# Sums of k over the tokens: 32x32 block transposes and a matmul of 8 columns in place of a matmul of 256 columns

## The chip, the cores and the metric

The kernel runs on one core of one Trainium2 chip, in float32. The metric is the device time of one execution in microseconds (us). Of the kernel before, four runs gave a median of 1077.0 us. One more execution was profiled, and all readings of the profile below are from that one.

## The reference

One transformer block over x of shape (16, 512, 256): 16 sequences, which the kernel calls batches, of 512 tokens with 256 features. A layer norm feeds a linear attention with 16 heads of 16 features and, beside it, a mixture of experts (a shared SwiGLU network, and two of eight experts for each token).

```python
x = L0_attn_inputs_q
xn = _layernorm(x, axis=-1)
...
q = _feature_map(q)          # elu(x) + 1
k = _feature_map(k)
kv = jnp.einsum('bkhd,bkhm->bhdm', k, v)
out = jnp.einsum('bqhd,bhdm->bqhm', q, kv)
normalizer = jnp.einsum('bqhd,bkhd->bqh', q, k)
normalizer = jnp.maximum(normalizer, EPS)
out = out / normalizer[..., None]
...
x = x + attention(xn) + ffn(xn)
```

The normalizer needs, for each batch, the sum of k over its 512 tokens: 256 numbers. These are the "sums of k" of the title. The same 256 numbers also carry the bias of v into kv.

## The kernel before, in words

Tokens lie on the 128 partitions: a batch is four tiles of 128 tokens by 256 features, so `kk` (the keys after the feature map) is 128x4x256. The loop over the 16 batches is software-pipelined by hand. In the body for batch b the program text has: `front(b+1)` (projections of k and q, feature maps, routing), `summarize(b)` (the products of k and the normalized x), `normalize(b+2)`, `hidden_rows(b)` (first layer of the routed experts, line 424), then `key_sum(b+1)` and `attend(b+1)`, `hidden(b)` (first layer of the shared network, line 443), `mix(b)` and `gather(b)` (lines 482 to 535). Batch 0 has its own `front`, `key_sum` and `attend` ahead of that. After the loop 67 or more tiles of tokens, sorted by their pair of experts, are fetched by indirect DMAs and multiplied with the experts' second layer (line 703).

Each engine executes its own instructions strictly in one order, and that order is fixed when the program is built: a scheduler places instructions by the order of the program text, by what it reckons to be ready, and by free buffers. An instruction whose inputs come late is therefore found behind others that stand after it in the text. Matmul results go to a pool of six PSUM buffers (`ps_mm`); a buffer is free again when VectorE or ScalarE has read it.

The sums of k are made in `key_sum` (lines 453 to 462). GpSimd adds the four token tiles to one of 128x256 (lines 456 and 457, tile `k2`). TensorE multiplies it with a 128x128 matrix of ones (line 459, tile `pks`), which adds over the 128 partitions and leaves the 256 sums on each of the 128 partitions. VectorE copies the result out of PSUM (line 461, tile `ksb`). `ksb` has two readers: `attend` (line 510), which divides q by the normalizer, writes it to memory (line 522) and reads it back in blocks for a transpose (lines 236 and 242), and `mix` (line 489). All the elementwise work of the routing (lines 346 to 414) and the evictions of the hidden layers (lines 432 and 450) are on VectorE too.

A float32 matmul appears in the profile as two TensorE instructions, each with its own load of the 128x128 weights: the 16 matmuls of line 459 are 32 entries.

Of the kernel before, what the change touches and what calls it, by code (L numbers as in the profile page):

```python
# [10 lines left out]
FP = mybir.dt.float32  # L11
AF = mybir.ActivationFunctionType
ALU = mybir.AluOpType
AX = mybir.AxisListType

P = 128
# [5 lines left out]
def block_kernel(  # L22
# [29 lines left out]
    nc = tc.nc  # L52
    B, S, D = x.shape
# [28 lines left out]
    const = ctx.enter_context(tc.tile_pool(name="const", bufs=1))  # L82
# [5 lines left out]
    small = ctx.enter_context(tc.tile_pool(name="small", bufs=2))  # L88
    dram = ctx.enter_context(tc.tile_pool(name="dram", bufs=1, space=bass.MemoryType.DRAM))
    ps_mm = ctx.enter_context(tc.tile_pool(name="ps_mm", bufs=6, space=bass.MemoryType.PSUM))  # L90
# [20 lines left out]
    Q = 32  # L111
    NQ = P // Q
# [7 lines left out]
    ident = const.tile([P, P], FP)  # L120
# [47 lines left out]
    def load_expert(i):  # L168
# [9 lines left out]
    ones = const.tile([P, P], FP)  # L178
# [6 lines left out]
    nc.gpsimd.affine_select(  # L185
        out=headmask, in_=headmask, pattern=[[DH, P // DH], [0, DH]],
        compare_op=ALU.is_ge, fill=0.0, base=DH - 1, channel_multiplier=-1,
    )

    before = const.tile([P, P], FP)  # L190
# [262 lines left out]
    def key_sum(b, kk):  # L453

        k2 = one.tile([P, 2, D], FP, tag="k2", name=f"k2_{b}")
        nc.gpsimd.tensor_tensor(k2, kk[:, 0:2, :], kk[:, 2:4, :], ALU.add)  # L456
        nc.gpsimd.tensor_tensor(k2[:, 0, :], k2[:, 0, :], k2[:, 1, :], ALU.add)
        pks = ps_mm.tile([P, D], FP, tag="mm", name=f"pks_{b}")
        nc.tensor.matmul(pks, lhsT=ones, rhs=k2[:, 0, :], start=True, stop=True)  # L459
        ksb = work.tile([P, D], FP, tag="ksb", name=f"ksb_{b}")  # L460
        nc.vector.tensor_copy(ksb, pks)
        return ksb

    def summarize(b, xn, kk):
# [275 lines left out]
    for b in range(B):  # L740
# [12 lines left out]
        if b == 0:  # L753
            sums = key_sum(0, kk)
            queries[0] = attend(0, qq, sums)
# [7 lines left out]
        if b + 1 < B:  # L763
            sums = key_sum(b + 1, fronts[b + 1][2])
            queries[b + 1] = attend(b + 1, fronts[b + 1][1], sums)
# [17 lines left out]
    n = nc.values_load(  # L783
        filled, min_val=TT, max_val=TILES,
        skip_runtime_bounds_check_because="whole tiles for all tokens, a part of a tile more for a pair",
    )
# [58 lines left out]
```

## Time and profile before

| what | value |
|---|---|
| median of 4 runs (lowest, highest) | 1077.0 us (1074.64, 1081.7) |
| profiled execution, whole | 1078.83 us |
| its span, first to last instruction | 1077.1 us |
| mean granted TensorE clock | 0.997 of full speed |
| PE (matmul) busy | 1053.5 us, 98% of the span |
| PEld (weight load) busy | 625.7 us, 58% |
| DVE (VectorE) busy | 662.1 us, 61%, 1744 instructions |
| ACT (ScalarE) busy | 376.0 us, 35% |
| POOL (GpSimd) busy | 243.9 us, 23% |

PE is the TensorE's matmul row and PEld its weight loads, which run beside the matmuls. Matmuls are pipelined: the duration of one (592 ns with 512 columns, 379 ns with 256) contains a latency that overlaps with the next, so that what one costs is read from the distance to the next one's start or from the chain of waits, not from its duration. "issue" in a list of waits is idle time for which the profile shows no cause.

### The profile page before, as it was taken

How to read it: one execution, taken by the hardware profiler on the slowest of the kernel's cores; microseconds unless marked ns; L12 is line 12 of the kernel's file. 1: busy time of each engine (PE TensorE's matmuls, PEld its weight loads, DVE VectorE, ACT ScalarE, POOL GpSimd, SP SyncE). 2: the span in 40 equal slices, each digit the busy share in tenths (PEclk: the TensorE clock that was granted, in tenths of full speed). 3: DMA queues.
4: the chain of work that ended last, by engine and by line, in shares of the span. 5: the costliest groups of instructions: out<-in, count | busy, mean ns of one | idle time of the engine just before them, and what ended most of it. 6: DMA issues, size and time to landing. Idle time of an engine off the chain costs nothing.

```text
span 1077.1 us, 11307 instructions
## 1 busy us (share of the span) xinstructions
PE 1053.5 (98%) x3404; PEld 625.7 (58%) x3404; DVE 662.1 (61%) x1744; ACT 376.0 (35%) x703; POOL 243.9 (23%) x313
## 2 busy tenths in 40 slices
PE   6999999999999999999999999999999999999996
PEld 5565747475757566665757474757566444444442
DVE  7948475565647474747474655646386576666663
ACT  3412231322232231313131322212112686777771
POOL 6102021010202020201011110102002665555552
PEclk9999999999999999999999999999999999999998
DMA  7343332424334242423232313031212654454440
GB/s 229 99 118 111 85 123 74 137 59 137 96 100 126 81 137 63 142 59 98 68 109 59 117 40 118 31 106 50 73 55 88 206 175 151 152 154 151 148 153 29
DMA packets 129054, 116.02 MB, mean 108 GB/s; under 512 B 72109, under 2 KB 113597, under 8 KB 128736
## 3 DMA queue, kind: packets, MB, share of 16 engines
q1 hardware_dynamic: 119120, 77.16, 23.7%
q0 software_dynamic: 9456, 37.59, 11.1%
q8 instruction: 29, 0.48, 0.2%
q10 hardware_dynamic: 416, 0.52, 0.2%
q14 instruction: 33, 0.27, 0.1%
HBM read 65.36 MB, written 50.27 MB: 107 GB/s over the span
## 4 chain that ended last, share of the span: by engine, by line
PE 94%; DVE 2%; DMA 1%; issue 1%; POOL 0%; ACT 0%; SPq 0%; POOLq 0%; DVEq 0%
PE phr L424 20%; PE phs L443 20%; PE py L703 19%; PE po L534 15%; PE pk L312 6%; PE pxk L469 5%; PE pq L323 5%; PE pm L499 2%; PE pvk L482 1%; PE pks L459 1%; DMA xn_all<-h_d,source 0%; DMA x<-in_x 0%; DMA kk_all<-h_d,source 0%; DMA qq_all<-h_d,source 0%; DVE hT L680 0%
## 5 line engine op out<-in xcount | busy, mean ns | idle before, releaser
L703 PE MATMUL py<-w_sb,hT 128*128 x536 | 230.5, 592 | 2.0 <-DVE hT L686 2.0
L443 PE MATMUL phs<-xnT,win_sb 128*128 128x512 f32 x512 | 223.6, 593 | 0.0
L424 PE MATMUL phr<-w_sb,xnT 128*128 128x512 f32 x512 | 222.8, 592 | 0.0
L703 PEld LDWEIGHTS py<-w_sb,hT 128*128 128x128 f32 x536 | 101.7, 190 | 130.5 <-issue 129.3
L424 PEld LDWEIGHTS phr<-w_sb,xnT 128*128 128x128 f32 x512 | 97.1, 190 | 114.7 <-issue 106.0
L443 PEld LDWEIGHTS phs<-xnT,win_sb 128*128 128x128 f32 x512 | 96.8, 190 | 113.2 <-issue 110.5
L292 POOL TENSOR_TENSOR res<-x,bo_sb 128x1024 f32<-128x1024 f32 x16 | 37.8, 2366 | 433.2 <-DMA h_d<-res 287.7
L534 PE MATMUL po<-wout_sb,hs_all 128*128 128x256 f32 x512 | 123.6, 379 | 0.0
L535 DVE TENSOR_TENSOR res<-po,res 128x256 f32<-128x256 f32 x64 | 27.2, 424 | 131.8 <-PE po L534 131.8
L534 PEld LDWEIGHTS po<-wout_sb,hs_all 128*128 128x128 f32 x512 | 96.1, 190 | 12.4
L450 DVE TENSOR_TENSOR hs_all<-phs,sa_hs 128x512 f32<-128x512 f32 x64 | 43.6, 681 | 91.8 <-PE phs L443 86.5
L449 ACT ACTIVATE sa_hs<-phs 128x512 f32<-128x512 f32 x64 | 38.2, 597 | 159.7 <-PE phs L443 154.4
L717 POOL DMA_INDIRECT out<-y,goal x67 | 67.6, 1009 | 76.3 <-DVE y L714 65.1
L301 ACT ACTIVATE km<-km 128x1024 f32<-128x1024 f32 x16 | 16.9, 1057 | 177.9 <-DVE km L300 177.9
L432 DVE TENSOR_TENSOR hr<-phr,sa_hr 128x512 f32<-128x512 f32 x64 | 43.8, 685 | 55.8 <-PE phr L424 32.8
L430 ACT ACTIVATE sa_hr<-phr 128x512 f32<-128x512 f32 x64 | 38.0, 597 | 99.1 <-PE phr L424 90.3
L534 PE MATMUL po<-kvo,qT 128*128 128x256 f32 x256 | 67.0, 384 | 0.0
L312 PE MATMUL pk<-wkr_sb,xnT 128*128 128x266 f32 x256 | 62.1, 396 | 3.9 <-DVE qq_all L327 2.3
L469 PE MATMUL pxk<-kk_all,xn_all 128*128 128x256 f32 x256 | 57.9, 379 | 0.0
L323 PE MATMUL pq<-wq_sb,xnT 128*128 128x256 f32 x256 | 57.8, 379 | 0.0
L312 PEld LDWEIGHTS pk<-wkr_sb,xnT 128*128 128x128 f32 x256 | 49.7, 195 | 13.6 <-ACT xnT L283 2.4
L456 POOL TENSOR_TENSOR k<-kk_all 128x512 f32<-128x512 f32 x16 | 27.6, 1727 | 130.4 <-DVE sm L358 126.6
(148 smaller groups left out, 1262.9 us busy)
## 6 DMA issues: line engine op xcount, KB each, us to landing
h_d<-hr SPq DMA_DIRECT2D x64, 256.0 KB, 2.5
h_d<-res SPq DMA_DIRECT2D x64, 129.0 KB, 1.8
q_d<-qq_all SPq DMA_DIRECT2D x16, 512.0 KB, 2.8
qb<-q_d SPq DMA_DIRECT2D x64, 128.0 KB, 2.6
w_sb<-in_w SPq DMA_DIRECT2D x64, 128.0 KB, 3.4
x<-in_x SPq DMA_DIRECT2D x15, 512.0 KB, 4.1
xn_d<-xn_all SPq DMA_DIRECT2D x14, 512.0 KB, 3.0
xb<-xn_d SPq DMA_DIRECT2D x56, 128.0 KB, 3.1
```

Source lines behind the costliest of these rows:

```text
L312: nc.tensor.matmul(pk, lhsT=xnT[:, k, ts(t, P)], rhs=wkr_sb[:, k, :], start=(k == 0), stop=(k == KD - 1),)
L323: nc.tensor.matmul(pq[:, t, :], lhsT=xnT[:, k, ts(t2 + t, P)], rhs=wq_sb[:, k, :], start=(k == 0), stop=(k == KD - 1),)
L424: nc.tensor.matmul(ph, lhsT=xnT[:, k, ts(t, P)], rhs=w1_sb[:, k, ts(half, HID)], start=(k == 0), stop=(k == KD - 1),)
L430: nc.scalar.activation(sa, halves[0], AF.Silu)
L432: nc.vector.tensor_tensor(hr, halves[1], sa, ALU.mult)
L443: nc.tensor.matmul(ph, lhsT=win_sb[:, k, ts(half * KH + f, P)], rhs=xnT[:, k, :], start=(k == 0), stop=(k == KD - 1),)
L449: nc.scalar.activation(sa, halves[0], AF.Silu)
L450: nc.vector.tensor_tensor(h[:, f, :], halves[1], sa, ALU.mult)
L469: nc.tensor.matmul(pxk[:, c, :], lhsT=xn[:, t, ts(c, P)], rhs=kk[:, t, :], start=(t == 0), stop=(t == NT - 1),)
L534: nc.tensor.matmul(po, lhsT=a, rhs=w, start=(i == 0), stop=(i == len(parts) - 1))
L703: nc.tensor.matmul(py.rearrange("p j d -> p (j d)"), lhsT=self.hT[:, f, ts(j, P)], rhs=w2_sb[:, f, bass.ds(regs[i % TR], 2 * D)], start=(f ...
L717: stored = nc.gpsimd.indirect_dma_start(out=out_rows, out_offset=bass.IndirectOffsetOnAxis(ap=self.goal[:, i : i + 1], axis=0), in_=y, in_ ...
```

## The change

`key_sum` adds over the partitions in another way. VectorE transposes each 32x32 block of the 128x256 tile (8 blocks in each of 4 groups of 32 partitions, which are called quadrants here): afterwards partition j of a quadrant holds, for each block n, the 32 tokens of that quadrant for feature 32n+j. VectorE adds these 32 and gets 128x8. A matmul with a constant 0/1 matrix `fold` (128x128, one where row and column agree modulo 32) adds the four quadrants and leaves the result in all four: 8 columns in place of 256. VectorE copies these 8 columns out of PSUM and then spreads them with a second block transpose, whose source repeats each column 32 times, to the same 128x256 tile `ksb` as before. `fold` is made once, at the start, by VectorE from the identity matrix.

```diff
+    fold = const.tile([P, P], FP)
+    nc.vector.tensor_reduce(fold[:, 0:Q], ident.rearrange("p (a j) -> p j a", j=Q), AX.X, ALU.add)
+    nc.vector.tensor_copy(
+        fold[:, Q:].rearrange("p (a j) -> p a j", j=Q), fold[:, 0:Q].unsqueeze(1).to_broadcast([P, NQ - 1, Q])
+    )
...
         nc.gpsimd.tensor_tensor(k2[:, 0, :], k2[:, 0, :], k2[:, 1, :], ALU.add)
-        pks = ps_mm.tile([P, D], FP, tag="mm", name=f"pks_{b}")
-        nc.tensor.matmul(pks, lhsT=ones, rhs=k2[:, 0, :], start=True, stop=True)
+        N = D // Q
+        nc.vector.transpose(
+            k2[:, 1, :].rearrange("p (n j) -> p n j", j=Q), k2[:, 0, :].rearrange("p (n j) -> p n j", j=Q)
+        )
+        kq = small.tile([P, 2, N], FP, tag="kq", name=f"kq_{b}")
+        nc.vector.tensor_reduce(
+            kq[:, 0, :], k2[:, 1, :].rearrange("p (n j) -> p n j", j=Q), AX.X, ALU.add
+        )
+        pks = ps_mm.tile([P, N], FP, tag="mm", name=f"pks_{b}")
+        nc.tensor.matmul(pks, lhsT=fold, rhs=kq[:, 0, :], start=True, stop=True)
+        nc.vector.tensor_copy(kq[:, 1, :], pks)
         ksb = work.tile([P, D], FP, tag="ksb", name=f"ksb_{b}")
-        nc.vector.tensor_copy(ksb, pks)
+        nc.vector.transpose(
+            ksb.rearrange("p (n j) -> p n j", j=Q), kq[:, 1, :].unsqueeze(2).to_broadcast([P, N, Q])
+        )
```

Here P is 128, D is 256, Q is 32 and NQ is 4. Nothing else of the kernel is edited.

## The prediction

> **What bounds the kernel now.** I read the page's chain of waits first, then the chain in order of time over one batch, then single instructions around the matmul that is replaced. The page's chain, by engine and by line, and two rows of the 40 slices:
>
> ```profile
> PE   6999999999999999999999999999999999999996
> DVE  7948475565647474747474655646386576666663
> ...
> PE 94%; DVE 2%; DMA 1%; issue 1%; POOL 0%; ACT 0%; SPq 0%; POOLq 0%; DVEq 0%
> PE phr L424 20%; PE phs L443 20%; PE py L703 19%; PE po L534 15%; PE pk L312 6%; PE pxk L469 5%; PE pq L323 5%; PE pm L499 2%; PE pvk L482 1%; PE pks L459 1%; DMA xn_all<-h_d,source 0%; DMA x<-in_x 0%; DMA kk_all<-h_d,source 0%; DMA qq_all<-h_d,source 0%; DVE hT L680 0%
> ```
>
> TensorE sets the end, and between the first slice and the last it has no visible hole: the busy times by stage give 704.00 us of 704.00 from 76 to 780 us. The idle time is at the start (9.6 us of the first 33 and 1.7 us at 73 us) and after 800 us. The replaced matmul, line 459, is a link of the chain. In order of time (start, duration, what):
>
> ```profile
> 136.27 13.73 PE phr L424 x32
> 150.00 0.43 PE pks L459 x2
> 150.43 13.73 PE phs L443 x32
> 164.16 0.89 PE pvk L482 x8
> ```
>
> It takes 0.431 us of TensorE per batch (two entries; 16 entries of 256 columns on line 323 take 3.45 us, 0.2156 each), 16 x 0.431 = 6.9 us in all. That is the most the change could win on TensorE. VectorE is busy 61% and has about 20 us free in each steady batch (31.13 us busy of 50.75 from 125.80 to 176.55).
>
> **What is saved on TensorE.** Eight columns don't cost an eighth of 32: weights are loaded for each entry. The nearest row is the routing's short matmul with 12 columns, once in the kernel, between matmuls of 256 columns:
>
> ```profile
> 785.26 0.41 PEld L545 LDWEIGHTS pc<-total,before 128*128 128x128 f32 x2
> 785.48 0.29 PE L545 MATMUL pc<-total,before 128*128 128x12 f32 x2
> 785.59 0.30 PEld L546 LDWEIGHTS pc<-total,ones 128*128 128x128 f32 x2
> 785.62 0.37 PE L546 MATMUL pc<-total,ones 128*128 128x12 f32 x2
> 785.81 0.52 PEld L469 LDWEIGHTS pxk<-kk_all,xn_all 128*128 128x128 f32 x3
> ```
>
> Weight loads of 0.19 us start at 785.48, 785.59, 785.70 (the second of the two that begin at 785.59) and 785.81: 0.11 us apart, with nothing long enough in between to hide them. The chain gives the four matmuls 0.12 + 0.22 us, and the 16 of line 469 behind them 3.55 us where others take 3.45, so 0.44 us for four, again 0.11 each. Line 482 above agrees: 8 entries of 128 columns in 0.89 us. A pair of 8 columns: 0.22 us. Bounds: 0.11, if one of the two loads is hidden after all, and 0.43, if it is no shorter than now. I take 0.22, by the row that it is nearest to. The saving is 16 x (0.431 - 0.22) = **3.4 us**, with ends of 0 and 5.1.
>
> [...]
>
> **What is added on VectorE**, per batch, with these rows (busy us, mean ns, then idle time before it):
>
> ```profile
> L512 DVE TENSOR_REDUCE rz<-qk 128x64 f32<-128x1024 f32 x16 | 19.4, 1214 | 0.4
> L686 DVE STREAM_TRANSPOSE hT<-hb 128x256 f32<-128x256 f32 x99 | 37.1, 420 | 6.4 <-ACT hb L673 5.3
> L317 DVE TENSOR_TENSOR lg<-pk,bkr_sb 128x10 f32<-128x10 f32 x64 | 10.0, 156 | 0.0
> L461 DVE COPY ksb<-pks 128x256 f32<-128x256 f32 x16 | 6.6, 415 | 6.2 <-PE pks L459 6.2
> L410 DVE TENSOR_REDUCE res<-parts 128x4 f32<-128x48 f32 x32 | 4.9, 195 | 0.0
> ```
>
> Two transposes of 128x256: 0.42 each; the second reads a repeated column, which no row shows, between 0.15 (a short instruction) and 1.24 (line 242, four times the size), taken at 0.42. The reduction of 256 numbers, between line 410 (48 in, 195 ns) and line 512 (1024 in, 1214 ns): 195 + 208 x 1019/976 = 412 ns. The copy of 8 columns from PSUM: 0.16 (10 columns, line 317). Less the old copy, 0.415. Sum 0.42 + 0.41 + 0.16 + 0.42 - 0.415 = **1.00 us per batch, 16 us in all**; VectorE goes from 662 to 678 us. Cost on the path: nothing, because some 20 us per batch are free there; if VectorE set the pace, it would be all 16 us.
>
> [...] One operation becomes four, one a reduction. If VectorE bounded the kernel, the sum would be 16 - 3.4 = 12.5 us slower by it; the chain above, 94% PE and 2% DVE, says that it doesn't.
>
> **The new wait.** The matmul used to need only GpSimd's sum; now it also waits for VectorE's transpose and reduction. Behind it on TensorE stand the 32 entries of line 443, and behind those all the rest, so any lateness goes straight to the end. How much room is there? Around the same link of the chain (start, duration, engine, line; last bracket: idle before it):
>
> ```profile
> 138.85 0.72 POOL L457 TENSOR_TENSOR k<-k 128x256 f32<-128x256 f32 x1
> ...
> 146.67 0.69 DVE L432 TENSOR_TENSOR hr<-phr,sa_hr 128x512 f32<-128x512 f32 x1 [0.20 <-PE phr L424]
> 150.47 0.42 DVE L461 COPY ksb<-pks 128x256 f32<-128x256 f32 x1 [3.10 <-PE pks L459]
> ```
>
> GpSimd's sum is there at 139.6, the matmul starts at 149.84. VectorE is full until 147.36 and then idle for 3.1 us: the two new operations (0.83 us) fit there with 1.6 us to spare. A batch later there is more: sum at 188.61, VectorE idle from 194.69 to 197.44, matmul at 200.60. VectorE's order is not the text's (the statistics of line 263 stand between evictions of line 432 that precede or follow them at will), so I expect such holes to be used. Cost 0, ends 0 and 1.9 us per batch (first rival).
>
> After the matmul the result is about 0.2 us later than before (0.16 + 0.42 against 0.415). Line 510 and the write of q (157.00 in this batch) move by that and by up to 0.8 us of the new operations; behind the write on SP's queue stand the four reads of line 236 (159.78), which land some 2.6 us after the last is issued, by 164.3, and are first used by the transpose of line 242 at 182.97: 18 us of cover. The PSUM buffer of `pks` comes free earlier, after a copy of 0.16 instead of 0.415.
>
> **The start.** `fold` costs a reduction of 128 numbers (0.28 by the same line) and a copy (0.2; at most 0.42) on VectorE, once. VectorE is idle until 2.85 us and again 0.78 and 0.87 us before its next two statistics, each waiting for x; the identity is ready at 2.75. Cost 0, at most 0.5. For batch 0 there is less cover: VectorE has no hole above 0.4 us from 6 to 57 us. There the copy of line 461 starts only at 35.98 though its matmul ran from 32.45 to 32.88. If the matmul kept its place and the two operations stood where the copy stands, TensorE would wait from 32.45 to 36.8, 4.4 us; if it moves behind some matmuls of line 424, nothing. PSUM buffers are another cover: at 46.62 TensorE needs one that line 432 frees at 44.3, so a VectorE that is 1 us later still frees it in time, one 2.3 us later doesn't. I take 0.5, ends 0 and 4.4.
>
> **Sum**: -3.4 + 0.5 = -2.9 us against the profiled span: 1077.1 becomes 1074.2, its execution 1078.83 becomes 1075.9. That execution stands 1.8 us above the median of the four runs; the same difference on the median gives 1077.0 - 2.9 = **1074.1 us**. The four runs spread from 1074.64 to 1081.7, 0.65%, so I count less than 0.5% (5.4 us) as no change.
>
> **Rivals.**
>
> Slower: the two VectorE operations stand behind the last eviction of line 432 while the matmul keeps its place. In the batch with the matmul at 200.60 that eviction ends at 201.55, the two operations at 202.4 and the matmul starts at about 202.5: 1.9 us of idle TensorE, 16 x 1.9 - 3.4 = +27 us, **1104 us**. It decides from 0.55 us per batch on, (5.4 + 3.4)/16. For it: in that batch the copy of line 461 stands just behind that eviction. Against it: the operations' input is there 12 us earlier, and one scheduler places both queues, which would put the matmul behind some of line 443.
>
> No gain: the first batch costs 2 to 4.4 us as worked out above and eats the saving: -3.4 + 3.4 = **1077 us**. For it the solid VectorE row at the start, against it that TensorE had other work to go on with (line 424).
>
> Faster than I say: one load of each pair hides (-5.1), and a shifted order closes the hole of 1.67 us before 74.78, where TensorE waits for a transpose of line 242 that stands behind an eviction of line 535: -6.8, **1070.2 us**. The four short matmuls at 785 us speak against the first half.
>
> The change doesn't do what it says: the short pair takes as long as the long one: **1077 us**. The spacing of 0.11 us speaks against it.
>
> **How the numbers follow.** Forecast 0.57, slower rival 0.14, no gain 0.13, faster rival 0.13, no shorter matmul 0.03. Faster by over 0.5% is the faster rival, 0.13; slower is the slower rival, 0.14; the other three cases, 0.73, are within. The range of 8 in 10 goes from 1070 (the faster rival's time) to 1082 (where the slower rival begins to count) and leaves out that rival and half of the faster one. The likeliest case alone: 1072 to 1076.
>
> **What would show it.** Right: the pair of line 459's successor takes about 0.22 us in the chain, the period from one batch's line 424 to the next's shrinks from 50.76 to about 50.55 us, and DVE busy rises by 16 us with PE as full as before. Wrong: idle time of PE or PEld before `pks` put down to the new reduction; a first matmul of line 424 later than 32.9 us; a pair at 0.43 us; or a batch period that grows.

## The result, and the profile after

| | before | after |
|---|---|---|
| median of the timed runs | 1078.05 us (71 runs) | 1079.78 us (44 runs) |
| lowest to highest | 1074.05 to 1082.69 | 1078.01 to 1082.7 |
| profiled execution, span | 1078.83, 1077.1 us | 1081.27, 1079.5 us |
| granted TensorE clock, profiled | 0.997 | 0.994 |
| DVE busy, instructions | 662.1 us, 1744 | 672.8 us, 1794 |

The ratio is 1.0019, with a 95% interval from 1.001 to 1.0027: slower by 1.1 to 2.9 us, where 2.9 us less were forecast. Less than 0.5%, and on the other side. The medians hide a change of form. Before, 32 of 71 runs lie below 1077; after, none of 44 lies below 1078.0. The slow end has not moved. The short times have gone.

The profile of after, the page's chain of waits by engine:

```profile
PE 92%; DVE 4%; DMA 2%; issue 1%; POOL 1%; SPq 0%; ACT 0%; POOLq 0%; DVEq 0%
```

TensorE still sets the end, but VectorE has gone from 2% to 4% of the chain. The chain of waits in order of time shows where. First one steady batch (start, duration, what):

```profile
141.29 13.73 PE phr L430 x32
155.03 0.12 PE pks L475 x2
155.15 13.84 PE phs L449 x32
168.98 0.89 PE pvk L501 x8
```

The short pair costs 0.12 us, and the 32 matmuls behind it 13.84 instead of 13.73: 0.23 us in all against 0.43 before. The period from one batch to the next goes from 50.76 to 50.55 us (`phr` starts at 242.24, 292.79 and 343.34). This is the forecast saving, and it is there in every steady batch.

The loss is all in the first 80 us. TensorE's timeline there, before and then after (start, duration, engine, line, tiles, shapes, count; last bracket: idle time before it and what ended it):

```profile
21.71 3.83 PE L312 MATMUL pk<-wkr_sb,xnT 128*128 128x266 f32 x16 [2.25 <-DVE qq_all L327]
25.38 3.62 PE L323 MATMUL pq<-wq_sb,xnT 128*128 128x256 f32 x16
28.83 3.62 PE L469 MATMUL pxk<-kk_all,xn_all 128*128 128x256 f32 x16
32.29 0.59 PE L459 MATMUL pks<-k,ones 128*128 128x256 f32 x2
32.72 13.90 PE L424 MATMUL phr<-w_sb,xnT 128*128 128x512 f32 x32
```

```profile
21.81 5.51 PE L318 MATMUL pk<-wkr_sb,xnT 128*128 128x266 f32 x16 [2.76 <-DVE qq_all L333]
27.16 3.62 PE L329 MATMUL pq<-wq_sb,xnT 128*128 128x256 f32 x16
30.61 3.62 PE L488 MATMUL pxk<-kk_all,xn_all 128*128 128x256 f32 x16
36.17 0.36 PE L475 MATMUL pks<-kq,fold 128*128 128x8 f32 x2 [1.94 <-DVE kq L471]
36.38 15.68 PE L430 MATMUL phr<-w_sb,xnT 128*128 128x512 f32 x32
```

Three differences: the 16 matmuls `pk` take 5.51 instead of 3.83 us, there is a wait of 1.94 us in front of `pks` for the new reduction, and the 32 matmuls `phr` take 15.68 instead of 13.90. They add to 0.1 + 1.7 + 1.9 + 1.8 = 5.5, less 0.2 for each of the two short pairs in that stretch. At the first `pk` of batch 2 the kernel is 80.01 - 74.78 = 5.2 us late. At `phr` of batch 14 it is 747.77 - 745.42 = 2.35 late: the 13 pairs in between won back 2.9, 0.22 each. The span ends 2.4 late.

The two longer groups are matmuls at half clock. Two windows of after (stretch, its length, busy time and instructions of PE, PEld, DVE, ACT and POOL, granted clock, DMA share, GB/s):

```profile
22.80:26.20 3.40, 3.40 (x9) 2.64 (x8) 3.40 (x11) 1.06 (x1) 2.54 (x2) 0.50 0.43 149
36.50:40.00 3.50, 3.50 (x6) 1.47 (x6) 3.48 (x11) 0.94 (x1) 2.45 (x2) 0.52 0.00 0
```

Each of the two holes is followed by 3.4 us at a granted clock of 0.50, which costs half of that, 1.7 us. PE is "busy" throughout, so neither its busy time (1053.3 us) nor its 98% shows anything. Before has the clock at 1.00 in both places. Only the second of the two belongs to the change, though: the first hole and a half clock behind it are found below in a kernel with the old matmuls too, so that 1.7 of the 5.2 us are luck of this pair of executions. The mean clock tells the same: 2 x 1.7 / 1079.5 = 0.003, which is 0.997 against 0.994.

Why is the reduction late? The chain of after, in order of time, just before the wait:

```profile
34.26 0.60 DVE qm L306
34.86 0.10 DVE ex L355
34.96 0.08 DVE ex L358
35.04 0.35 DVE k L467
35.39 0.31 DVE st L269
35.70 0.33 DVE kq L471
36.03 0.14 issue
36.17 0.36 PE pks L475 x2
```

GpSimd's sum, the transpose's input, is ready at 26.1 us. The transpose (L467) starts 8.9 us later. It stands on VectorE behind routing of the first batch and evictions and feature maps of the second, and VectorE has only one gap there, of 0.45 us.

### The profile page after: what moved, and what is told of

Same layout as the page of the kernel before. It is cut to its first block, busy times and chain, and to the rows that moved or that the text cites. A ratio compares the mean times of both kernels' runs of the same rounds, so it can differ in the third digit from the quotient of the medians.

```text
span 1079.5 us, 11287 instructions
## 1 busy us (share of the span) xinstructions
PE 1053.3 (98%) x3404; PEld 625.5 (58%) x3404; DVE 672.8 (62%) x1794; ACT 376.2 (35%) x703; POOL 244.9 (23%) x313
## 4 chain that ended last, share of the span: by engine, by line
PE 92%; DVE 4%; DMA 2%; issue 1%; POOL 1%; SPq 0%; ACT 0%; POOLq 0%; DVEq 0%
PE phr L430 20%; PE phs L449 20%; PE py L722 19%; PE po L553 15%; PE pxk L488 5%; PE pk L318 5%; PE pq L329 4%; PE pm L518 1%; PE pvk L501 1%; DMA x<-in_x 1%; DMA xn_all<-h_d,source 0%; DMA kk_all<-h_d,source 0%; DMA qq_all<-h_d,source 0%; DVE hT L699 0%; POOL qq_all L673 0%
```

## The experiments

The theory: all of the loss is in batch 0, where the matmul now waits for a full VectorE queue; the wait itself and the half clock behind it cost more than the 16 short pairs save. Rivals: the loss comes from the later batches (shifted order, more VectorE work), or from `fold` at the start. The first four kernels ran on one chip (before there: median 1083.27 us of 30 runs), the other four on another (before there: 1077.2 us of 35 runs), and each ratio is against before on the same chip.

**Batch 0 in the old form, the rest in the new one.**

```diff
+        if b > 0:
...
+        else:
+            pks = ps_mm.tile([P, D], FP, tag="mm", name=f"pks_{b}")
+            nc.tensor.matmul(pks, lhsT=ones, rhs=k2[:, 0, :], start=True, stop=True)
+            ksb = work.tile([P, D], FP, tag="ksb", name=f"ksb_{b}")
+            nc.vector.tensor_copy(ksb, pks)
```

> Batch 0 adds over the partitions by the matrix of ones as before, batches 1 to 15 in the new way. Theory A (the loss is TensorE's wait for the reduction of batch 0 and the half clock behind it; every later batch gains 0.2 us): no idle time before the first matmul of pks, the first matmul of phr at about 33 us, time 3.0 us below the kernel before (15 x 0.2), ratio about 0.997. Rival B (the 16 us more on VectorE, or the making of fold at the start, cost the time): ratio at or above 1.000, and the lateness is there without the wait.

Measured: 1078.79 us (12 runs), ratio 0.9967, interval 0.9948 to 0.9985. The loss is gone and the saving shows. So the later batches aren't where the time is lost, nor is `fold`, which is still made here. One thing shows up that had been hidden: `pks` of batch 1 waits 0.86 us for its reduction. After has no wait there, with TensorE some 6 us later at that point.

**Only batch 0 in the new form.**

```diff
-        if b > 0:
+        if b == 0:
```

> Only batch 0 adds in the new way, batches 1 to 15 as before. Theory A: the whole loss and almost none of the gain: TensorE idle some 1.9 us before the first pks, a half clock of 3.4 us after it in most runs (1.7 us), so 4 to 5.5 us above the kernel before, ratio 1.004 to 1.005. Rival B: the time of the kernel before or 1 us more.

Measured: 1090.1 us (7 runs), ratio 1.0058, interval 1.0033 to 1.0083, so 3.6 to 9 us for a single matmul. The two ratios multiplied give 0.9967 x 1.0058 = 1.0025, the changed kernel's own (1.0019 and, on the second chip, 1.0024): within their intervals, the two parts make up the whole. TensorE's timeline of this kernel:

```profile
27.07 3.62 PE L494 MATMUL pxk<-kk_all,xn_all 128*128 128x256 f32 x16
35.29 0.57 PE L476 MATMUL pks<-kq,fold 128*128 128x8 f32 x2 [4.61 <-DVE kq L472]
35.71 16.32 PE L430 MATMUL phr<-w_sb,xnT 128*128 128x512 f32 x32
```

TensorE is 3.5 us earlier than in after (`pxk` at 27.07, not 30.61), because the first hole was only 0.53 us in this run. It gains little: the reduction lets `pks` start only 0.9 us earlier, so the wait grows to 4.61 us, and the 32 `phr` behind it, at half clock at first (0.65 granted from 35.7 to 42.5 us, 1.00 from there to 50), take 16.32 instead of 13.90 us. What TensorE gains at the start is lost again at this wait.

**All batches new, the first sum and its matmul moved behind half of `phr`.** `hidden_rows` calls a function between its second and third token tile, which makes the sum and `attend` of batch 0.

```diff
         for t in range(NT):
+            if t == 2:
+                halfway()
...
-        if b == 0:
-            sums = key_sum(0, kk)
-            queries[0] = attend(0, qq, sums)
...
+        def halfway():
+            if b == 0:
+                first.append(key_sum(0, kk))
+                queries[0] = attend(0, qq, first[0])
```

> All batches in the new way, but the sums and the normalizer of batch 0 stand behind the second token tile of its hidden rows in the program text, so that TensorE has four matmul groups of phr to do before it needs the reduction. Theory A: no idle time before the first pks, ratio about 0.997, the same as with batch 0 in the old way. Rival B: no change against the changed kernel, 1.002. A third way, that the later normalizer of batch 0 makes its q late: idle time before the po matmuls of batch 0, ratio above 1.000.

Measured: 1080.68 us (12 runs), ratio 0.9976, interval 0.9956 to 0.9996. With all 16 sums in the new form the kernel is faster than before, by 0.4 to 4.8 us, once TensorE has something to do in place of the wait. TensorE's timeline:

```profile
33.95 7.03 PE L432 MATMUL phr<-w_sb,xnT 128*128 128x512 f32 x16
40.81 0.28 PE L477 MATMUL pks<-kq,fold 128*128 128x8 f32 x2
40.95 7.11 PE L432 MATMUL phr<-w_sb,xnT 128*128 128x512 f32 x16
```

`phr` starts right behind `pxk`, no idle time stands ahead of `pks`, and the 32 `phr` take 14 us, not 15.7. The first hole (2.33 us) and its half clock (`pk` takes 5.52 us) are still there.

**The changed kernel, with the hole in front of `pks` filled.** Four unused matmuls, 8 entries, are added between `pxk` and `pks` in batch 0; their results are read by nobody. `last_pxk`, not shown, holds the last matmul of `pxk`.

```diff
...
+        if b == 0:
+            pw = ps_mm.tile([P, D], FP, tag="mm", name="pw")
+            with tc.issue_after(last_pxk[0].ins):
+                for _ in range(4):
+                    nc.tensor.matmul(pw, lhsT=ident, rhs=xn_all[:, 0, 0, :], start=True, stop=True)
```

> The changed kernel with four extra matmuls of 256 columns (1.7 us, their result is not used) between the last pxk and the first pks of batch 0: TensorE works through the time in which it would be idle. If idle TensorE is followed by a half clock, as the trace of the changed kernel suggests, the clock stays full in the window of 34 to 40 us, the 32 matmuls of phr of batch 0 take 13.7 us instead of 15.5, and the time falls by up to 1.7 us against the changed kernel: ratio to the kernel before 1.000 to 1.001. If the half clock has another cause, it stays at 1.002.

Measured: 1083.84 us (12 runs), ratio 1.0012, interval 0.9988 to 1.0037. The interval holds both the changed kernel's ratio and one below 1, so the time tells nothing. The trace does, first TensorE's timeline and then the window of `phr`:

```profile
34.79 1.89 PE L480 MATMUL pw<-xn_all,ident 128*128 128x256 f32 x8
36.90 0.36 PE L482 MATMUL pks<-kq,fold 128*128 128x8 f32 x2 [0.21 <-DVE kq L473]
37.11 13.98 PE L430 MATMUL phr<-w_sb,xnT 128*128 128x512 f32 x32
```

```profile
37.00:51.00 14.00, 14.00 (x34) 6.09 (x34) 13.99 (x53) 7.08 (x9) 3.80 (x7) 1.00 0.21 77
```

With the hole filled and nothing else changed, the clock stays at 1.00 and `phr` takes 13.98 instead of 15.68 us. So in this execution no half clock followed. Alone that doesn't show the idle time to be the cause, because the last kernel of this section has a hole of 1.90 us and no half clock behind it either; what tells the cases apart is worked out in the next section.

**Before, with `fold` added and nothing else.** Its result is read by nobody.

```diff
+    fold = const.tile([P, P], FP)
+    nc.vector.tensor_reduce(fold[:, 0:Q], ident.rearrange("p (a j) -> p j a", j=Q), AX.X, ALU.add)
+    nc.vector.tensor_copy(
+        fold[:, Q:].rearrange("p (a j) -> p a j", j=Q), fold[:, 0:Q].unsqueeze(1).to_broadcast([P, NQ - 1, Q])
+    )
```

> The kernel before, and beside it the two VectorE operations that make fold (not used for anything). Theory A: they stand between the statistics and the normalization of batch 1, 0.5 us where TensorE is still busy with q of batch 0, and cost nothing: ratio 0.999 to 1.001. Rival B (making fold at the start is what costs): ratio 1.002 or more and a longer idle time of TensorE before the keys of batch 1.

Measured: 1077.78 us (12 runs), ratio 0.9996, interval 0.9976 to 1.0015: no cost that can be measured. The profiled execution, 1082.23 us, has a first hole of 3.95 us, and the `pk` behind it take 6.66 instead of 3.83 us (granted clock 0.50 from 22 to 28 us), though all its matmuls are the old ones. Before has the hole without `fold` (2.25 us), and here VectorE had also waited 1.78 us for the x of batch 1. So the first hole isn't the change's doing.

**Batches 0 and 1 old, 2 to 15 new.**

```diff
+        if b > 1:
...
+        else:
```

The program text also makes `fold` later here, behind `normalize(1)`, and so does that of the next kernel. On VectorE it stands where it stood, between the statistics and the normalization of batch 1 (10.73 us here, 11.39 in after).

> Batches 0 and 1 in the old way, 2 to 15 in the new one. Theory A: also the 0.9 us that TensorE waited for the reduction of batch 1 when only batch 0 was old is gone; 14 x 0.2 = 2.8 us gained, no idle time before any pks, ratio about 0.996 to 0.997. Rival B: not below 1.000.

Measured: 1073.56 us (12 runs, nine of them from 1072.21 to 1074.32), ratio 0.9971, interval 0.9955 to 0.9987. It beats both kernels: 3.6 us less than before and 6.6 us less than the changed kernel on the same chip, from giving up two of 16 savings. In the profiled execution (1072.21 us, span 1070.4) there is no first hole, and `phr` starts at 29.03 us:

```profile
18.09 3.77 PE L313 MATMUL pk<-wkr_sb,xnT 128*128 128x266 f32 x16
...
29.03 13.90 PE L425 MATMUL phr<-w_sb,xnT 128*128 128x512 f32 x32
```

Against before's span that is 32.72 - 29.03 = 3.7 us from the start and 14 x 0.21 = 2.9 from the short pairs: 6.6 of the 6.7 us. The first part comes from this execution having no first hole, which the edit isn't shown to bring about: the medians differ by 3.6 us, not 6.7.

**The same, and GpSimd's residual of batches 0 and 1 issued behind their routing.** This asks whether the first hole comes from GpSimd (see the last section).

```diff
...
+        if b > 1:
+            add()
         qq, kk, lg = project(b, xnT)
-        route(b, lg, res)
+        last = route(b, lg, res)
+        if b <= 1:
+            with tc.issue_after(last.ins):
+                add()
```

> As the kernel with batches 0 and 1 in the old way, and GpSimd adds the output bias to x of batches 0 and 1 only after their routing, not while VectorE makes their softmax. If the 2.3 us of the small subtractions of the routing at 16 to 21 us are a wait for GpSimd's additions (their ends coincide in the traces), they take 0.2 us here, TensorE's idle time before the keys of batch 1 falls under 0.5 us, no half clock follows in any run, and the time falls by another 1 to 4 us: ratio about 0.994. If not, the 2.3 us stay.

Measured: 1075.21 us (12 runs), ratio 0.9976, interval 0.9963 to 0.9988. The spread shrinks to 1072.84 to 1075.97, from 1072.21 to 1078.42: no run is as slow as the slowest three of the kernel above, which fits slow starts made by GpSimd. In the profile the two subtractions take 0.19 and 0.16 us and the first hole is gone, as expected, but so it is in the profile of the kernel above, with the addition in its old place. The expected fall of another 1 to 4 us didn't come; the median is 1.7 us higher. The profile has a new wait of 0.66 us in front of `phs` (for the eviction in line 438), and the rest of the difference to the kernel above is open.

**The changed kernel again, unedited, on the second chip.**

> The changed kernel once more, unedited, on the chip of the three others, as their measure. Theory A: TensorE waits for the reduction of batch 0 again, 1.9 us if there was idle time before the keys of batch 1, some 4.6 us if there was none (VectorE reaches the reduction at 35 to 36 us either way); ratio 1.001 to 1.003.

Measured: 1080.17 us (12 runs, 1078.09 to 1081.62), ratio 1.0024, interval 1.0012 to 1.0036. TensorE's timeline:

```profile
21.53 5.51 PE L318 MATMUL pk<-wkr_sb,xnT 128*128 128x266 f32 x16 [2.60 <-DVE qq_all L333]
...
35.84 0.36 PE L475 MATMUL pks<-kq,fold 128*128 128x8 f32 x2 [1.90 <-DVE kq L471]
36.06 13.98 PE L430 MATMUL phr<-w_sb,xnT 128*128 128x512 f32 x32
```

The wait is back (1.90 us). This time no half clock follows it (1.00 granted from 36 to 50 us), and the span is 1076.3 against 1079.5. The wait belongs to the changed kernel; the half clock behind it comes in some executions.

## Why the prediction was wrong

**The step that failed** is "The start": "I take 0.5, ends 0 and 4.4". As the change of batch 0 alone it measured 3.6 to 9 us. In the profiled pair it is 1.9 us of waiting and 1.8 us of half clock, and the 1.7 us behind the first hole come on top. The working held the right place: "If the matmul kept its place and the two operations stood where the copy stands, TensorE would wait from 32.45 to 36.8". The matmul kept its place, and started at 36.17. It was chosen against because TensorE "had other work to go on with (line 424)". But in batch 0 `pks` stands on TensorE ahead of all 32 of line 424, where in steady batches it stands behind them, and in the 1.94 us before `pks` of after TensorE ran no matmul. That order was in the trace of before. The rival "No gain" named this mechanism, and in size it was still short.

**What no step had** is the clock. A hole of about 2 us may cost 1.7 us more afterwards, in matmuls that look busy. With a short first hole this takes the start past the upper end of 4.4: in the kernel with only batch 0 new the wait is 4.61 us and `phr` takes 16.32 - 13.90 = 2.4 us more. The half clock came after holes of 1.94, 2.31 to 2.33, 2.60 and 2.76 us, and not after holes of 1.90 and 2.25. Ahead of the end of the program, the stretches at half clock last 3.41 or 6.83 us, the longer ones after holes of 3.95 and 4.61 us, and of 5.2 to 6.0 us near 865 us in the four kernels on the first chip.

What tells 1.94 from 2.25 us is where a hole lies. In all ten traces every stretch at full clock is a whole number of steps of 3.41 us long (10.24 and 1034.24 us in after, 3 and 303 steps). Counted back from each halving of the clock, the last of these steps had TensorE idle for 57% of its time or more, in all 21 cases, ten of them at the end of the program; of the other 3069 steps at full clock none had more than 50%. First the hole of 1.94 us in after, then that of 1.90 us in the changed kernel on the second chip (stretch, its length, busy time of PE, granted clock, DMA share, GB/s; each first line is the step with most of the hole, the second the step behind it):

```profile
33.00:36.41 3.41, 1.48 (x9) 1.00 0.00 0
36.41:39.83 3.42, 3.42 (x6) 0.50 0.00 0
```

```profile
32.08:35.49 3.41, 1.87 (x9) 1.00 0.00 0
35.49:38.90 3.41, 3.06 (x9) 1.00 0.00 0
```

The hole of 1.94 us lies within one step, 57% of which is idle. That of 1.90 us is cut in two, 45% and 10% of a step, and so is the 2.25 us of before, 16% and 50%. With the hole filled, the step from 34.20 to 37.61 us is busy for 3.20 us; without the four matmuls the 1.94 us from 34.96 to 36.90 would have lain in it. The steps fall differently in each execution: the first recorded stretch at full clock begins 10.9 to 13.7 us into the span. So a hole of some 2 us costs 1.7 us more or nothing, by luck. All this is read from the traces afterwards; no run was made to test it.

**What held.** The short pair: 0.22 forecast, 0.23 measured, from the spacing of 0.11 us. The saving: 50.55 us was forecast as the new period, and measured. The new VectorE work was priced at 1.00 us per batch. It measured 1.03, less the old copy, as the groups of after by line show (busy us, mean ns, idle before it):

```profile
L467 DVE STREAM_TRANSPOSE k<-k 128x256 f32<-128x256 f32 x16 | 6.9, 434 | 0.6 <-POOL k L463 0.6
L471 DVE TENSOR_REDUCE kq<-k 128x8 f32<-128x256 f32 x16 | 6.6, 414 | 0.0
L476 DVE COPY kq<-pks 128x8 f32<-128x8 f32 x16 | 2.5, 156 | 12.9 <-PE pks L475 12.9
L478 DVE STREAM_TRANSPOSE ksb<-kq 128x256 f32<-128x256 f32 x16 | 7.0, 439 | 0.3
```

The row's total rose by 10.7, not by 16: other VectorE instructions took less in that execution. In after it is hidden, from batch 1 on (with batch 0 old, batch 1 waited 0.86 us). So is the new wait: the list of waits has one wait of `pks` for VectorE in the whole kernel, the first, so the rival "Slower" didn't occur.

```profile
PE pks L475 <- DVE kq L471: 1.9, 1, 1.9
PE pk L318 <- DVE xnT L248: 1.7, 1, 1.7
```

The last of these is the hole before batch 2, unchanged at 1.7 us, so the rival "Faster" didn't occur either. `fold` costs nothing that can be measured.

**What stays open.** How often the half clock follows each hole in the runs without a profile isn't known, since those leave only a mean clock. And the time of the kernel with the hole filled wasn't told apart from the changed kernel's.

## What to carry to other kernels

A dependency moved to another engine has to be checked where that engine's queue is fullest, here in the first pass, and there by the order in which the waiting engine takes its own work: one wait of 2 to 4.6 us, with the half clock that may follow, ate what 16 shorter matmuls saved. A steady saving can be kept by leaving the first passes in the old form, or by putting other work ahead of the wait. And a group of matmuls that takes longer than its twin while "busy" is to be read with the granted clock beside it.

## What the runs showed of the hardware

Half clock (0.50 granted for 3.41 us) after idle times as short as 1.94 us is told above. The other surprise is the first hole, up to 3.95 us before `pk` of batch 1, in before and after alike. It goes with two tiny VectorE subtractions that share a stretch with a large GpSimd addition. The timeline of after:

```profile
16.44 2.36 DVE L355 TENSOR_TENSOR ex<-lg,mx 128x32 f32<-128x32 f32 x1
18.71 2.35 DVE L358 TENSOR_TENSOR ex<-lg,mx 128x8 f32<-128x8 f32 x1
```

```profile
16.36 4.67 POOL L298 TENSOR_TENSOR res<-x,bo_sb 128x1024 f32<-128x1024 f32 x2 [2.80 <-DMA bo_sb<-in_bo]
```

And the kernel with batches 0 and 1 old:

```profile
15.88 0.19 DVE L350 TENSOR_TENSOR ex<-lg,mx 128x32 f32<-128x32 f32 x1
15.99 0.16 DVE L353 TENSOR_TENSOR ex<-lg,mx 128x8 f32<-128x8 f32 x1
...
16.22 5.69 POOL L293 TENSOR_TENSOR res<-x,bo_sb 128x1024 f32<-128x1024 f32 x2 [2.03 <-DMA bo_sb<-in_bo]
```

Ahead of GpSimd's addition the two take 0.19 and 0.16 us; beside it 2.36 and 2.35, each as long as one GpSimd addition (4.67 / 2), and the second ends with the second addition, at 21.06 and 21.03 us. So an instruction of 0.16 us took as long as a whole one of GpSimd; what holds it up isn't shown. GpSimd's idle time before the addition, 2.80 us in after, ends with the load of `bo_sb`, so which of the two comes first is a race of some tenths of a microsecond (GpSimd at 16.36 and VectorE at 16.44 us in after, 16.22 and 15.88 in the other kernel). The ten traces line up: in six both subtractions are caught and the hole is 2.25 to 3.95 us; in the two kernels on the first chip that changed batch 0 alone or left it alone only the first is caught and the hole is 0.53 and 0.74 us; in the two with no subtraction caught there is none. The narrow spread with the residual moved fits this race being a large part of the kernel's spread. In the changed kernel it matters less who wins it, because the wait for the reduction at 35 to 36 us takes back most of what an early start had won.
